# Gated cross-attention with a sparse FFN on one core: four engines in written order, and work placed between the seven products of each stage

## The chip, the core and the metric

The kernel runs on one core of a Trainium2 chip. A core has a matrix engine (TensorE, PE in the profile; its weight loads are listed as PEld), a vector engine (VectorE, DVE), a scalar engine (ScalarE, ACT), a general engine (GpSimd, POOL) and an engine that here issues nearly all data transfers (SyncE, SP). The metric is the device time of one execution in microseconds (us); several runs are given by their median.

## What is computed

The input x is 32 sequences of 64 tokens with 512 channels (2048 tokens). With `ctx` of the same shape, a bias and a mask per sequence:

```python
# cross-attention: 32 heads of 128
q = layernorm(x) @ Wq ; k = ctx @ Wk ; v = ctx @ Wv
score = where(mask, q k^T / sqrt(128) + bias, -inf)
x = x + tanh(g_xattn) * ((softmax(score) v) @ Wo)
# FFN on y = layernorm(x), 1792 hidden units in 56 blocks of 32
inter = y @ c1^T @ c2^T
idx = first argmax of each block of inter
x = x + tanh(g_ffn) * (relu(y . w1[idx]) @ w2t[idx])
```

The FFN is computed densely: all 1792 hidden values, each multiplied by 1 where it is the first maximum of its block and by 0 elsewhere.

## The kernel before

**Products by Strassen's scheme.** Each 512x512x512 product is done as seven products of half-size blocks instead of eight. The class `Seven` holds a matrix as four raw blocks and three sums of blocks: `sums_left` (L129) makes the sums of a weight on POOL, four operations that each read two SBUF operands; `sums_right` (L139) makes those of the other operand on DVE, also four. `product` (L156) writes one of the seven into a PSUM bank of the tag "mm" (four banks); it is eight matmul instructions in the trace, and a stage of seven is 56. `collect` (L172) adds a finished product to the result: the first is copied by ACT (L177), the others are added by DVE (L179 to L190), eight operations in a stage. The order is `ORDER = (0, 5, 1, 6, 4, 2, 3)`; `RAW_FIRST = (0, 1, 5, 6, 4, 2, 3)` begins with the two products that use raw blocks alone.

**Attention** runs over 4 blocks of 512 tokens and in each over 8 groups of 4 heads: 32 units, u = 0 to 31. A unit has the stages q and k (`project_q`, L284), `values` of the unit before (po, L378), `scores` (sc, L325), v, and `output_sums` of the unit before (pw, L400), whose seven products are summed over the groups of a block in `acc` (L401; for a block's first group ACT copies them, L399). Inside k, ahead of its fifth product, stands `transpose_probs` of the unit before (pt, L109; ACT copies the result, L365). `scores` adds the bias on DVE (L332), takes the maximum (L341), subtracts it (L342), has ACT take the exponential (L345), and DVE sums (L346), inverts (L347), masks (L349) and multiplies (L355). At a block's end POOL combines the seven sums (`finish_sums`, L407 to L413) and DVE adds the result to x (`finish_block`, L418). In a block's last unit the next block of x is normalised and transposed (`norm_block`, L277) and the next `ctx` is loaded.

**FFN**: for each of the 4 blocks of tokens, `ffn_rank` (pc, L458) and `ffn_eq` (pi, L485) compute `inter` in two small products, DVE takes each block's maximum (L498) and compares (L499), POOL multiplies by a rank (L500), DVE takes the maximum again (L503) and POOL subtracts (L504), so that the first maximum is left over. `ffn_hidden` (L511 to L567) computes the hidden units in four groups (512, 512, 512 and 256) as seven chains of matmuls each; `ffn_output` (fo, L582) multiplies by w2. pi uses the two PSUM banks of the tag "pv", from block 1 on also two of "mm".

**Order.** `manual_schedule` (L195) names PE and POOL: these two carry out their instructions in the order in which they are written. DVE, ACT and SP are ordered by the framework's scheduler, which may put an instruction ahead of one that is written earlier. Weights have one buffer each (tags wq, wk, wv, wo): the next unit's weight is issued on SP when the stage that used the buffer is over, and POOL makes its sums when it has landed. The bias tile has two buffers; POOL adds the mask to it (L303) in the unit that uses it. The first loads are issued on SP in the order ctx, wk, wv, x.

Of the kernel before, what the change touches and what calls it, by code (L numbers as in the profile page):

```python
# [23 lines left out]
P = 128  # L24
# [11 lines left out]
def kernel(  # L36
# [54 lines left out]

    def stats_of(pool, t0, n, name):
        st = pool.tile([P, n, 6], F32, tag=f"bnst{n}", name=f"st_{name}")
        mv = pool.tile([P, n, 2], F32, tag=f"bnmv{n}", name=f"mv_{name}")
        for i in range(n):
            nc.vector.bn_stats(st[:, i, :], xacc[:, t0 + i, :])
            nc.vector.bn_aggr(mv[:, i, :], st[:, i, :])
        return mv, rstd_of(pool, mv, n, f"rstd_{name}")
# [96 lines left out]
    with tc.manual_schedule(engines={mybir.EngineType.PE, mybir.EngineType.Pool}):  # L195

        def load_weight(tag, g):
            w = seven(wpool, tag, f"{tag}_{g}")
            src = {"wq": wq_d, "wk": wk_d, "wv": wv_d}.get(tag)
            if src is None:  # L200
                src = wo_d[ts(g % NHG, HG * DH), :]
            else:
                src = src[:, ts(g % NHG, HG * DH)]
            nc.sync.dma_start(w.raw, src.rearrange("(c p) n -> p c n", p=P))
            return w.sums_left(nc.gpsimd)

        def load_ctx(b):
            c = seven(att, "cT", f"cT_{b}")
            nc.sync.dma_start(
                c.raw, ctxT_d[:, ts(b, 512)].rearrange("(c p) t -> p c t", p=P)  # L210
            )
            return c

        make_identity(nc, ident)
        nc.vector.tensor_copy(identb, ident)
        nc.vector.memset(eps, EPS)
        nc.scalar.dma_start(gate[:, 0:1], gx_d.partition_broadcast(P))
        nc.scalar.dma_start(gate[:, 1:2], gf_d.partition_broadcast(P))
        nc.scalar.activation(tgx, gate[:, 0:1], AF.Tanh)
        nc.scalar.activation(tgf, gate[:, 1:2], AF.Tanh)  # L220

        cT = load_ctx(0)
        W = {"wk": load_weight("wk", 0), "wv": load_weight("wv", 0)}
        load_x(0, 2)
        load_x(2, 2)
        W |= {t: load_weight(t, 0) for t in ("wq", "wo")}
        for t in range(4, NTILE, 4):
            load_x(t, 4)
# [24 lines left out]
        class Norm:  # L253


            def __init__(self, b, name):
                self.b, self.name = b, name
                self.mv, self.rstd = stats_of(att, 4 * b, 4, f"{name}{b}")
                self.xn = {}

            def scale(self, *tiles):
                for i in tiles:
                    self.xn[i] = normalise(
                        att, 4 * self.b + i, self.mv, self.rstd, i, f"{self.name}{self.b}_{i}"
                    )

            def turn(self, *tiles):
                if 0 in tiles:
                    self.xT = seven(att, "xT", f"{self.name}xT_{self.b}")
                for i in tiles:  # L270
                    pt = ps_tr(f"{self.name}xt_{self.b}_{i}")
                    transpose4(pt, self.xn[i])
                    nc.scalar.copy(
                        self.xT.raw[:, :, ts(i, P)], pt.rearrange("p (k t) -> p k t", k=KC)
                    )

        def norm_block(b):  # L277
            n = Norm(b, "a")
            for i in range(4):
                n.scale(i)  # L280
                n.turn(i)
            return n.xT.sums_right(nc.vector)

        def project_q(u, w, src, name, mid=None, order=None):  # L284
            dst = att.tile([P, 2, 2, 512], F32, tag=name, name=f"{name}_{u}")
            pp = {}
            for n, i in enumerate(order or ORDER):
                if n == 4 and mid is not None:
                    mid()
                pp[i] = product(i, w, src, f"{name}_{u}_{i}", name != "v")  # L290
                if i == 1 and 5 not in pp:
                    continue
                collect(i, pp[i], dst)
                if i == 5 and 1 in pp:
                    collect(1, pp[1], dst)
# [17 lines left out]
        def scores(u, b, q, k, bt):  # L313
# [31 lines left out]
            nc.scalar.activation(pf, pf, AF.Exp)  # L345
            nc.vector.tensor_reduce(st[:, 1, :], pr, AX.X, ALU.add)  # L346
# [11 lines left out]
            return pf  # L358
# [34 lines left out]
        def output_sums(u, g, w, oT, acc, mid=None):  # L393
            for n, i in enumerate(ORDER):
                if n == 4 and mid is not None:
                    mid()
# [18 lines left out]
        def finish_block(b, acc):  # L415
            for i, r, half in ((1, 0, 0), (2, 0, 1), (3, 1, 0), (4, 1, 1)):
# [16 lines left out]
        def ffn_constants():  # L433
# [15 lines left out]
            nc.vector.tensor_copy(rank, rank_i)  # L449
            F.update(c2T=c2T, c1T=c1T, i1=i1, rank=rank)  # L450

        def ffn_rank(b):

            xT, i1 = F["norm"].xT, F["i1"]
            pc = ps_tr(f"pc_{b}")
# [15 lines left out]
        def ffn_eq(b, g, tiles, banks):  # L471
# [24 lines left out]
            for i, pi, ef in zip(tiles, pis, efs):  # L496
# [3 lines left out]
                nc.gpsimd.tensor_tensor(ef, ef, F["rank"][:, :n], ALU.mult)  # L500
            for i, ef in zip(tiles, efs):
# [18 lines left out]
        def ffn_hidden(b, g, mid1=None, mid2=None):  # L520
# [22 lines left out]
            nc.scalar.copy(h[0][1], view(X))  # L543

# [64 lines left out]

        cT.sums_right(nc.vector)  # L610
        k = project_q(0, W["wk"], cT, "k", order=RAW_FIRST)
        W["wk"] = load_weight("wk", 1)
        n = Norm(0, "a")
        n.scale(0, 1)

        def turn_first():
            n.turn(0, 1)
            n.scale(2, 3)
            n.turn(2, 3)

        v = project_q(0, W["wv"], cT, "v", turn_first, order=RAW_FIRST)
        xT = n.xT.sums_right(nc.vector)
        W["wv"] = load_weight("wv", 1)
        madd, seen = mask_block()
        prev = None
        acc = None
        U = NB * NHG
        done = None
        for u in range(U):
            b, g = divmod(u, NHG)  # L630
            mid = None
            if prev is not None:
                mid = lambda: transpose_probs(prev[0], prev[4])

            def queries(mid=None):
                q = project_q(u, W["wq"], xT, "q", mid)
# [6 lines left out]
            def keys(mid=None):  # L643
                k = project_q(u, W["wk"], cT, "k", mid)
# [6 lines left out]
            if u == 1:  # L651
                k = keys()
                q = queries(mid)
            else:
                q = queries()
                bt = load_bias(g, b)
                if g == NHG - 1 and b + 1 < NB:
                    xT = norm_block(b + 1)
                if u > 0:
                    k = keys(mid)  # L660
            if u == 1:
                bt = load_bias(g, b)
            if prev is not None:
                oT = values(prev[0], prev[3])
            if done is not None:
                finish_block(*done)
                done = None
            if u == U - 1:
                F["norm"] = Norm(0, "f")
                F["norm"].scale(0, 1)  # L670
            pf = scores(u, b, q, k, bt)
            if u > 0:
                v = project_q(u, W["wv"], cT, "v")
            if g == NHG - 1 and b + 1 < NB:
                cT = load_ctx(b + 1).sums_right(nc.vector)
            if u == U - 1:
                ffn_weight(2)
                ffn_constants()
                F["norm"].turn(0, 1)
                F["norm"].scale(2, 3)  # L680
            elif u > 0:
                W["wv"] = load_weight("wv", u + 1)
            if prev is not None:
                pu, pb, pg = prev[:3]
                if pg == 0:
                    acc = att.tile([P, 7, 512], F32, tag="acc", name=f"acc_{pb}")
                output_sums(
                    pu,
                    pg,
                    W["wo"],  # L690
                    oT,
                    acc,
                    (lambda: F["norm"].turn(2, 3)) if u == U - 1 else None,
                )
                if pg == NHG - 1:
                    finish_sums(acc)
                    done = pb, acc
                W["wo"] = load_weight("wo", u)
            prev = (u, b, g, v, pf)

        pv2 = (ps_pv, ps_pv)
        low, high = (0, 1), (2, 3)
        ffn_rank(0)
        transpose_probs(U - 1, pf)
        oT = values(U - 1, v)
        ffn_eq(0, 0, low, pv2)
        output_sums(U - 1, NHG - 1, W["wo"], oT, acc, lambda: ffn_eq(0, 0, high, pv2))
        ffn_weight(3)
        for b in range(NB):
            for g in range(4):  # L710
                m1 = m2 = None
                if b == 0 and g < 3:
                    m1 = lambda: ffn_eq(0, g + 1, low, pv2)
                    m2 = lambda: ffn_eq(0, g + 1, high, pv2)
                elif b > 0 and g < 2:
                    m1 = lambda: ffn_eq(b, 3, (low, high)[g], pv2)
                if g == 3 and b + 1 < NB:
                    F["norm"] = Norm(b + 1, "f")
                    F["norm"].scale(0, 1)
                ffn_hidden(b, g, m1, m2)  # L720
                if b == 0 and g == 0:
                    finish_sums(acc)
                    ffn_weights2(0)
                if b == 0 and g == 1:
                    finish_block(NB - 1, acc)
# [6 lines left out]
            more = b + 1 < NB  # L732
# [4 lines left out]
            for g in range(3):  # L737
                if more:
                    ffn_eq(b + 1, g, low + high, (ps_mm, ps_mm, ps_pv, ps_pv))
                if g < 2:  # L740
                    ffn_output(b, g + 2)
# [49 lines left out]
```

## Time and profile before

| | |
|---|---|
| median of 3 runs | 2267.83 us (2266.33 to 2271.6) |
| profiled execution, its own time | 2270.99 us |
| its span in the trace | 2269.2 us |
| mean granted TensorE clock | 0.989 |
| first matmul | 10.7 us into the span |
| PE busy | 2218.4 us, 98% |
| DVE, POOL, ACT busy | 53%, 41%, 15% |
| moved by DMA | 173.57 MB |

In the profile's lines a group of instructions is given as line, engine, operation, out<-in by the program's names, shapes and count; a timeline line begins with the start and the length in us, and ends, in brackets, with the engine's idle time before it and what ended it. A line of waits reads "engine line waited for: us in total, times, longest us". A line of the windows view gives a stretch, its length and the busy time and number of instructions of PE, PEld, DVE, ACT and POOL in it, then the granted TensorE clock (1 is full), the DMA engines' busy share and GB/s.

### The profile page before, as it was taken

What the parts mean: (1) busy time and instruction counts of PE and PEld (TensorE: products, weight loads), DVE (VectorE), ACT (ScalarE), POOL (GpSimd) and SP (SyncE); (2) the same over time, 40 slices, a digit from 0 to 9 for tenths busy, and PEclk for the clock granted to TensorE, in tenths of its full rate; (3) what the DMA queues carried; (4) which work ended last, traced back from release to release, by engine and by line L of the source; (5) the groups of instructions that cost most, each with busy time, mean ns of one, the idle gap of its engine ahead of it and who ended that gap; (6) DMA issues with size and microseconds to landing.
All of it is one profiled execution on the core that took longest, in us unless ns stands there. A gap on an engine that the chain in (4) does not pass through costs nothing.

```text
span 2269.2 us, 29536 instructions
## 1 busy us (share of the span) xinstructions
PE 2218.4 (98%) x12336; PEld 1857.3 (82%) x12336; DVE 1203.3 (53%) x1745; ACT 351.7 (15%) x572; POOL 931.8 (41%) x724
## 2 busy tenths in 40 slices
PE   7999999999999999999999999999999989999999
PEld 6788888888888888888888888888888865656574
DVE  6545555754555557545555565455555774545451
ACT  1211111211111112121111121211111211112020
POOL 5443344454344444544444445343334462313130
PEclk9999999999999999999999999999999999999999
DMA  6222222222222222222222232222222220000000
GB/s 246 75 84 84 88 95 87 102 84 66 89 95 87 84 84 103 84 82 86 84 84 84 84 103 84 84 84 84 87 94 80 65 75 10 10 13 7 15 5 19
DMA packets 88516, 173.57 MB, mean 76 GB/s; under 512 B 4480, under 2 KB 4992, under 8 KB 88384
## 3 DMA queue, kind: packets, MB, share of 16 engines
q1 hardware_dynamic: 87440, 171.19, 22.6%
q8 instruction: 98, 1.61, 0.3%
q10 hardware_dynamic: 944, 0.49, 0.1%
q14 instruction: 34, 0.28, 0.0%
HBM read 167.48 MB, written 4.19 MB: 76 GB/s over the span
## 4 chain that ended last, share of the span: by engine, by line
PE 92%; POOL 3%; DVE 2%; DMA 2%; issue 1%; ACT 0%; SPq 0%; POOLq 0%
PE v L163 17%; PE k L163 17%; PE q L163 16%; PE pw L163 15%; PE fo L582 9%; PE po L378 5%; PE hx L511 4%; PE sc L325 3%; PE hz L511 2%; PE pt L109 1%; PE hy L511 1%; PE pi L485 1%; DMA wv<-in_dram 1%; DVE xacc L418 1%; DMA wq<-in_dram 0%
## 5 line engine op out<-in xcount | busy, mean ns | idle before, releaser
L163 PE MATMUL q<-axT,wq 128*128 128x256 f32 x1792 | 400.9, 384 | 11.7 <-DVE q L179 9.6
L163 PE MATMUL k<-cT,wk 128*128 128x256 f32 x1792 | 399.1, 380 | 12.8 <-DMA wk<-in_dram 10.7
L163 PE MATMUL v<-wv,cT 128*128 128x256 f32 x1792 | 397.3, 382 | 1.9 <-DVE v L179 1.9
L163 PEld LDWEIGHTS q<-axT,wq 128*128 128x128 f32 x1792 | 344.8, 193 | 62.3 <-issue 14.3
L163 PE MATMUL pw<-wo,oT 128*128 128x256 f32 x1792 | 392.5, 379 | 0.0
L163 PEld LDWEIGHTS k<-cT,wk 128*128 128x128 f32 x1792 | 338.9, 191 | 58.1 <-issue 10.7
L163 PEld LDWEIGHTS v<-wv,cT 128*128 128x128 f32 x1792 | 338.9, 191 | 49.5 <-DVE v L179 2.3
L163 PEld LDWEIGHTS pw<-wo,oT 128*128 128x128 f32 x1792 | 340.2, 190 | 47.6 <-issue 0.8
L401 DVE TENSOR_TENSOR acc<-pw,acc 128x512 f32<-128x512 f32 x196 | 134.2, 690 | 156.6 <-PE pw L163 156.4
L132 POOL TENSOR_TENSOR wv<-wv 128x512 f32<-128x512 f32 x32 | 41.4, 1295 | 378.0 <-DMA wv<-in_dram 365.7
L582 PE MATMUL fo<-w,hT 128*128 128x512 f32 x448 | 195.8, 594 | 0.0
L582 PEld LDWEIGHTS fo<-w,hT 128*128 128x128 f32 x448 | 83.9, 190 | 104.7 <-issue 102.2
L132 POOL TENSOR_TENSOR wq<-wq 128x512 f32<-128x512 f32 x32 | 42.6, 1332 | 225.2 <-DMA wq<-in_dram 192.0
L132 POOL TENSOR_TENSOR wk<-wk 128x512 f32<-128x512 f32 x32 | 48.0, 1499 | 188.1 <-DMA wk<-in_dram 157.5
L378 PEld LDWEIGHTS po<-pbd,v 128*128 128x128 f32 x1024 | 121.7, 192 | 3.4 <-ACT pbd L365 1.0
L378 PE MATMUL po<-pbd,v 128*128 128x128 f32 x1024 | 123.0, 278 | 0.6 <-ACT pbd L365 0.6
L132 POOL TENSOR_TENSOR wo<-wo 128x512 f32<-128x512 f32 x32 | 40.5, 1266 | 186.3 <-DMA wo<-in_dram 133.1
L500 POOL TENSOR_TENSOR eqa<-eqa,ffn_const 128x512 bf16<-128x512 bf16 x32 | 37.0, 1165 | 181.6 <-DVE eqa L499 180.9
L511 PE MATMUL hx<-fxT,w 128*128 128x256 f32 x448 | 109.2, 389 | 0.0
L511 PEld LDWEIGHTS hx<-fxT,w 128*128 128x128 f32 x448 | 87.3, 196 | 17.4 <-issue 4.9
L387 ACT COPY oT<-po 128x512 f32<-128x512 f32 x128 | 74.9, 585 | 159.0 <-PE po L378 158.9
L365 ACT COPY pbd<-pt 64x512 f32<-64x512 f32 x128 | 74.2, 579 | 159.5 <-PE pt L109 151.4
(144 smaller groups left out, 2528.4 us busy)
## 6 DMA issues: line engine op xcount, KB each, us to landing
wk<-in_dram SPq DMA_DIRECT2D x32, 1024.0 KB, 5.3
wv<-in_dram SPq DMA_DIRECT2D x32, 1024.0 KB, 5.5
wq<-in_dram SPq DMA_DIRECT2D x32, 1024.0 KB, 5.3
wo<-in_dram SPq DMA_DIRECT2D x32, 1024.0 KB, 5.4
bias<-in_dram SPq DMA_DIRECT2D x64, 256.0 KB, 2.8
cT<-in_dram SPq DMA_DIRECT2D x4, 1024.0 KB, 5.3
out_dram<-xacc SPq DMA_DIRECT2D x16, 256.0 KB, 2.0
w<-in_dram SPq DMA_DIRECT2D x2, 1792.0 KB, 8.4
```

Source lines behind the costliest of these rows:

```text
L109: nc.tensor.transpose(pt[:, ts(k, P)], src[:, ts(k, P)], ident)
L132: eng.tensor_tensor(s1, a21, a22, ALU.add)
L163: nc.tensor.matmul(pp[:, ts(j, HALF)], a[:, kc, ts(j, P)], b[:, kc, :], start=(kc == 0), stop=(kc == 1),)
L325: nc.tensor.matmul(sc[ts(r, S), ts(col, S)], q[:, hp, half, tok : tok + S], k[:, hp, half, tok : tok + S], start=True, stop=True,)
L365: nc.scalar.copy(pbd[ts(c, S), ts(half, 8), c, :], pt[ts(c, S), :].rearrange("p (a q) -> p a q", q=S),)
L378: nc.tensor.matmul(po[:, ts(2 * j + i, P)], v[:, r, half, i * HALF + j * P : i * HALF + (j + 1) * P], pbd[:, ((2 * half + i) * 2 + r) * 2 ...
L387: nc.scalar.copy(oT.raw[:, 2 * r : 2 * r + 2, ts(half, HALF)], po.rearrange("p (j t) -> p j t", j=2),)
L401: nc.vector.tensor_tensor(acc[:, i], pw, acc[:, i], ALU.add)
L418: nc.vector.scalar_tensor_tensor(a, acc[:, i].rearrange("p (i n) -> p i n", i=2), tgx, a, ALU.mult, ALU.add,)
L500: nc.gpsimd.tensor_tensor(ef, ef, F["rank"][:, :n], ALU.mult)
L511: nc.tensor.matmul(pp[:, ts(j, HALF)], s[:, kc, ts(j, P)], t[:, kc, :], start=(first and j == 0 and kc == 0), stop=(j == nj - 1 and kc == ...
L582: nc.tensor.matmul(po, F["hT", c // 4][:, c % 4, ts(i, P)], F["w2"][c // 7][:, c % 7, :], start=(c == 0), stop=(c == NIC - 1),)
```

## The change

All four compute engines follow the written order, and each stage takes a dictionary of hooks: work that is written ahead of its n-th product. `norm_block` and `stats_of` become the methods `stats`, `scale` and `turn` of `Norm`, spread over q and k of a block's last unit; `scores` ends with the exponential, and the rest, `divide`, stands ahead of v's third product; `finish_block` is cut into four parts in k and v; `ctx`'s sums move into q of the next block's first unit; the bias is loaded and masked one unit ahead; the last steps of `ffn_eq` (`ffn_first`) are put off until the next call or `ffn_ties`; the FFN's first `ffn_rank` and `ffn_eq` move into pw of unit 30; from block 1 on group 3's `ffn_eq` moves to later places; and the first ctx and wk are loaded in halves of their columns, wk from ACT's queue. The tanhs of the gates and the bf16 identity move behind unit 0's scores.

```diff
-    with tc.manual_schedule(engines={mybir.EngineType.PE, mybir.EngineType.Pool}):
+    with tc.manual_schedule(
+        engines={
+            mybir.EngineType.PE,
+            mybir.EngineType.Pool,
+            mybir.EngineType.DVE,
+            mybir.EngineType.Activation,
+        }
+    ):
...
+            if parts is None:
+                nc.sync.dma_start(w.raw, src)
+                return w.sums_left(nc.gpsimd)
+            for cols in parts:
+                nc.scalar.dma_start(w.raw[:, :, cols], src[:, :, cols])
+            return w
...
+        halves = (slice(0, HALF), slice(HALF, 512))
+        cT = load_ctx(0, halves)
+        W = {"wk": load_weight("wk", 0, halves)}
+        load_x(0, 4)
         make_identity(nc, ident)
         nc.vector.memset(eps, EPS)
+        W["wk"].sums_left(nc.gpsimd)
+        W |= {t: load_weight(t, 0) for t in ("wv", "wq", "wo")}
...
-        def project_q(u, w, src, name, mid=None, order=None):
...
+        def project(u, w, src, name, hooks=None, order=None):
+
             dst = att.tile([P, 2, 2, 512], F32, tag=name, name=f"{name}_{u}")
             pp = {}
             for n, i in enumerate(order or ORDER):
-                if n == 4 and mid is not None:
-                    mid()
+                call(hooks, n)
                 pp[i] = product(i, w, src, f"{name}_{u}_{i}", name != "v")
...
             nc.scalar.activation(pf, pf, AF.Exp)
+            return pf, pr, st
+
+        def divide(b, pr, st):
             nc.vector.tensor_reduce(st[:, 1, :], pr, AX.X, ALU.add)
...
+            ffn_ties()
+            F["ties"] = lambda: ffn_first(b, g, tiles, efs, nb, blocks, over)
...
+            hq, hk, hv, hp = {}, {}, {}, {}
             if prev is not None:
-                mid = lambda: transpose_probs(prev[0], prev[4])
+                turn_probs = lambda: transpose_probs(prev[0], prev[4])
+                (hq if u == 1 else hk)[4] = turn_probs
+            if last:
+                F["norm"] = norm = Norm(b + 1, "a") if more else Norm(0, "f")
+                for i in range(4):
+                    hq[i + 2] = lambda i=i: norm.stats(i)
+                hk[0] = lambda: norm.scale(0, 1)
+                hk[1] = lambda: norm.turn(0)
+                hk[2] = lambda: (norm.turn(1), norm.scale(2, 3))
+                hk[3] = lambda: norm.turn(2)
+                hk[5] = lambda: norm.turn(3)
+                if more:
+                    hp[1] = lambda: norm.xT.sums_right(nc.vector)
+                else:
+                    hp[4] = lambda: ffn_rank(0)
+                    hp[6] = lambda: ffn_eq(0, 0, low, pv2)
+            if g == 0 and u > 0:
+                hq[3] = lambda: cT.sums_right(nc.vector)
+            if done is not None:
+                hk[5] = lambda: finish_block(*ended, (0,))
+                hk[6] = lambda: finish_block(*ended, (1,))
+                hv[5] = lambda: finish_block(*ended, (2,))
+                hv[6] = lambda: finish_block(*ended, (3,))
...
+            pf, pr, st = scores(u, b, q, k, B_.pop(u))
+            bias(u + 1)
+            hv[2] = lambda: divide(b, pr, st)
             if u > 0:
-                v = project_q(u, W["wv"], cT, "v")
+                v = project(u, W["wv"], cT, "v", hv)
...
-        ffn_eq(0, 0, low, pv2)
-        output_sums(U - 1, NHG - 1, W["wo"], oT, acc, lambda: ffn_eq(0, 0, high, pv2))
-        ffn_weight(3)
+        ffn_eq(0, 0, high, pv2)
+        output_sums(
+            U - 1,
+            NHG - 1,
+            W["wo"],
+            oT,
+            acc,
+            {
+                2: lambda: ffn_eq(0, 1, low, pv2),
+                5: lambda: ffn_eq(0, 1, high, pv2),
+            },
+            RAW_FIRST,
+        )
...
+                    if g == 0:
+                        m1 = lambda: (ffn_eq(0, 2, low, pv2), ffn_weight(3))
+                        m2 = lambda: (
+                            ffn_eq(0, 2, high, pv2),
+                            finish_sums(acc),
+                            ffn_weights2(0),
+                        )
+                    if g == 2:
+                        m1 = lambda: finish_block(NB - 1, acc, (0, 1))
+                        m2 = lambda: finish_block(NB - 1, acc, (2, 3))
+                    ties = (0, 0, 2, 3)[g]
+                else:
+                    if g == 0:
+                        m2 = lambda: ffn_eq(b, 3, low, pv2)
+                    if g == 1:
+                        m1 = lambda: ffn_eq(b, 3, high, pv2)
+                        m2 = ffn_ties
+                if more and g == 3:
                     F["norm"] = Norm(b + 1, "f")
-                    F["norm"].scale(0, 1)
-                ffn_hidden(b, g, m1, m2)
+                    m1 = lambda: F["norm"].stats(0, 1, 2, 3)
+                    m2 = lambda: F["norm"].scale(0, 1)
+                ffn_hidden(b, g, m1, m2, ties)
```

## The prediction

> **What bounds the kernel now.** I read the page first, then what TensorE (PE) waits for, its clock over stretches, and the timeline of one unit. Section 1 of the page:
>
> ```profile
> PE 2218.4 (98%) x12336; PEld 1857.3 (82%) x12336; DVE 1203.3 (53%) x1745; ACT 351.7 (15%) x572; POOL 931.8 (41%) x724
> ```
>
> PE is the bound, and no matmul is removed. In a steady unit it has no gap: in the chain, v of units 5 and 6 starts at 312.13 and 367.24, 55.11 us apart, each 56-matmul stage 12.1 us, each of its seven products 1.73. Only PE's waits can be won. The longest, with us in total, times, longest:
>
> ```profile
> PE pi L485 <- DVE eqb L499: 16.8, 7, 7.6
> PE k L163 <- DMA wk<-in_dram: 10.7, 1, 10.7
> PE q L163 <- DVE q L179: 9.6, 3, 3.2
> ```
>
> A wait can cost more than its length. Two neighbouring stretches of unit 1 (PE busy, then PEclk, third from the right):
>
> ```profile
> 96.60:99.40 2.80, 0.90 (x5) 0.74 (x5) 2.77 (x4) 0.00 (x0) 0.00 (x0) 1.00 0.49 181
> 99.50:102.80 3.30, 3.30 (x9) 2.59 (x9) 3.30 (x7) 1.06 (x1) 0.00 (x0) 0.50 0.00 1
> ```
>
> After a wait of 1.90 us the clock is half for 3.4 us. The same view of the FFN: from the last attention sums to group 2; group 0 of block 1; its group 1:
>
> ```profile
> 1784.97:1866.70 81.73, 72.39 (x362) 56.11 (x361) 58.68 (x87) 17.78 (x30) 49.76 (x42) 0.94 0.26 83
> 1943.99:1964.99 21.00, 17.83 (x80) 14.17 (x77) 13.55 (x24) 4.20 (x6) 10.95 (x12) 0.84 0.04 13
> 1964.99:1978.86 13.87, 13.87 (x78) 11.72 (x77) 6.92 (x14) 4.20 (x6) 2.44 (x4) 1.00 0.00 0
> ```
>
> The stage on which I think the change turns is v. Unit 5, then unit 9, in the timeline:
>
> ```profile
> 311.75 1.44 POOL L132 TENSOR_TENSOR wk<-wk 128x512 f32<-128x512 f32 x1 [5.28 <-DMA wk<-in_dram]
> 311.99 1.76 DVE L145 TENSOR_TENSOR oT<-oT 128x512 f32<-128x512 f32 x1
> ...
> 312.06 12.35 PE L163 MATMUL v<-wv,cT 128*128 128x256 f32 x56
> ...
> 314.10 0.58 ACT L177 COPY v<-v 128x512 f32<-128x512 f32 x1 [3.35 <-PE v L163]
> ...
> 316.07 1.27 POOL L135 TENSOR_TENSOR wk<-wk 128x512 f32<-128x512 f32 x1
> 316.23 2.19 DVE L342 TENSOR_TENSOR prob<-prob,sst 128x1024 f32<-128x1024 f32 x1
> 318.35 0.68 DVE L179 TENSOR_TENSOR v<-v,v 128x512 f32<-128x512 f32 x1
> 318.52 1.06 ACT L345 ACTIVATE prob<-prob 128x1024 f32<-128x1024 f32 x1 [3.84 <-DVE prob L342]
> ```
>
> ```profile
> 541.97 0.68 DVE L145 TENSOR_TENSOR oT<-oT 128x512 f32<-128x512 f32 x1
> 542.18 1.60 POOL L132 TENSOR_TENSOR wk<-wk 128x512 f32<-128x512 f32 x1 [5.67 <-PE sc L325]
> ...
> 547.54 1.06 ACT L345 ACTIVATE prob<-prob 128x1024 f32<-128x1024 f32 x1 [2.88 <-DVE prob L342]
> ```
>
> See the copy of v's first product (L177) standing well ahead of the exponential, and a DVE operation with two SBUF inputs (L145, L342) waiting out the POOL operation in flight (2.19 us, where L355 of the same shape, free of POOL, takes 1.22). If POOL starts wk's sums before L145 (18 of units 1 to 31), the exponential comes 6.45 us after v's start; if after (13), 5.5.
>
> **The change part by part.**
>
> *v stage.* `scores` writes the exponential ahead of v, so ACT in written order can't copy v's first product until it is done; and DVE does the whole of `divide` before it collects the third. Four banks hold the products: the fifth needs the first's bank, the seventh the third's. Before, the fifth starts at 7.01 and the seventh at 10.46 us after v's start, unhindered. Late form: exponential at 6.45, copy behind it from 7.41 to 7.99, fifth product at 8.03: 1.02 lost. DVE then: collect (L179) at 8.02, sum (L346) at 8.62, reciprocal 1.25 later, then 0.28, 0.21 and 1.14 (spacings of unit 1's rows) to the collect at 11.50, done 12.18; seventh product at 12.22, not 11.48: 0.74. Sum 1.76. Early form: copy done at 7.03, so 0.06, then 0.74: 0.80. In all 18 x 1.76 + 13 x 0.80 = **+42.1**. Behind the waiting copy on ACT stands nothing else; DVE's collects wait for it. Units 7, 15 and 23 show a table load (1.28) between subtraction and exponential, and unit 31 now gets one, its square root having moved ahead: 4 x 1.28 = **+5.1**.
>
> Do these waits cool the clock? The Trainium skill ("TensorE: Matmul & The Clock Gate", Part 1: The HAM clock gate) has the clock fall only after an idle window of about 3.4 us: then no. The row above contradicts it, 1.90 us sufficed; yet a wait of 2.10 at 64.5 did not cool. Waits of 1.02 and 0.74 lie far under both: nothing. Units 7 and 31 wait about 2.3: half of 2 x 1.7 (3.4 us at half clock): **+1.7**; by the page 0.
>
> *Block ends.* v to v across units 8-9, 16-17, 24-25 takes 62.25, 62.39, 60.50 in the chain against 55.11: 19.8 too much, because DVE sits in `finish_block` (L418) for POOL's sums while q's products wait. Now its four parts stand in k and v of that unit, some 10 us after POOL's seven sums, one behind each product. The transposes' waits go too (3 x 0.46). **-21.2**. New is `cT.sums_right` in q of the next block's first unit: four two-input operations meet wo's four POOL sums (454.74 to 459.81 in unit 8) and alternate with them, about 1.25 + 0.6 each, so that q's fourth product is collected 1.7 us after k's first needs its bank: 3 x 1.7 = **+5.0**. The hooks in unit 7's q and k (statistics, scaling, transposes) leave DVE 1.6 us of work per 1.73 us product and stay inside the four-bank slack; xn may be 0.1 late: **+0.3**.
>
> *FFN.* Group 0 of blocks 1 to 3 takes 21.0, 20.4 and 19.5 us, an undisturbed group with one pair of pi 13.9: 19.3 lost to pi waiting for DVE's comparison and to the half clock after it. The pair moves some 8 us later, when DVE's four comparisons (5.6 us) are over: **-19.3**. Against it, group 3 of blocks 0 to 2 now holds the next block's statistics: DVE 4 x 0.92 from 0.85 us into the group, the square root on ACT to 4.9, and behind it on ACT the copy L543 that the sixth chain waits for: that at 5.25 instead of 3.96, and 0.43 more behind the Relu: 3 x 1.73 = **+5.2**.
>
> Transition: pw of unit 31 starts 23.8 us after pw of unit 30, as now (23.7). From there 12.1 for pw, 2.1 for two pi pairs and 1.4 for the first of them (its banks are still being compared), 15.3 for group 0, 14.3 for group 1: 45.2. DVE lags, but `finish_block` no longer stands before a pi. 23.8 + 45.2 = 69.0 against 81.7, less 0.9 of transposes moved into k: **-11.8**.
>
> *Start.* The first two products need only first halves. On one queue 1.02 MB had landed at 7.0 us and 2.07 MB at 10.0. A second queue (ACT) carries wk. The skill ("Trainium Kernel Development and Optimization", Key Constraints) says that queues share the same 16 engines and only issue time is saved: then PE starts at about 7.3, but the third product needs two POOL sums (1.3 each) of the whole wk, at 13.0 instead of 15.93: **-2.9**. If queues added up, about -5. A 512 KB load in 1 KB packets took 5.0 us beside another: then 0. Bias one unit ahead takes away POOL's late addition in units 0 and 1 (losses of 2.4 + 0.7 + 0.2 and 3.85); 1.1 comes back, since k of unit 1 waits behind unit 0's exponential and tanhs: **-6.0**.
>
> *At nothing.* Ties (`ffn_first`) deferred: POOL and DVE work behind chains that need it a group later; uncovered, one call's four reductions cost 2.8. `ffn_rank` comes 6.9 us into pw of unit 30, and its constants landed 6.9 us after issue on ACT's queue, behind which no product waits: 0.2 at most. w1's last group is loaded two pi later, needed three groups on. The second half of w2 is issued after `finish_block`'s last part: 8.4 us to land against about 12 of PE work; uncovered, 1 to 4. Bias on POOL after wk's sums: it ends 8.9 us into v, DVE's next two-input operation comes at 9.2. SP's order stays the scheduler's; the mask load could come late at 3 us. The moved pi, transposes and copies are the same instructions.
>
> Sum: 42.1 + 5.1 + 1.7 - 21.2 + 5.0 + 0.3 - 19.3 + 5.2 - 11.8 - 2.9 - 6.0 = **-1.8 us**. Span 2269.2 becomes 2267.4. The profiled execution took 2270.99, 1.8 outside the span, 3.2 above the median 2267.83. So the median becomes 2266.0.
>
> **Rivals.**
> 1. *Faster: the exponential in its early form everywhere.* wk's landing and L145 are 0.3 us apart; if wk lands a little later, all 31 units lose 0.80: 17 us less, 2249. Should wk's sums miss the softmax altogether, v's waits vanish and it is 2224. Against: SP issues wk at the same point of k.
> 2. *Slower: the late form everywhere.* The other side of the same 0.3 us: 13 x 0.96 = 12.5 more, 2278. It counts as slower from 25 late units of 31 on (7 more than 18: -1.8 + 6.7 = +4.9).
> 3. *Gains not had*: the hooks put as much DVE work before other banks. With half of the FFN's and blocks' 42 us (net) lost, 2287; with a quarter, 2276. For it: DVE is busy 58.7 of the transition's 81.7 us.
> 4. *It does nothing*: written order equals the scheduler's in q, k, pw. Against: L177 and L345 do change places.
>
> **How the numbers follow.** My forecast (-12 to +6 about -1.8) 0.45; rival 1 0.20; rival 2 0.12; rival 3 0.20; rival 4 0.03. Within 0.2% (4.5 us, about what a measurement tells from no change): 0.18 of the forecast, rival 4, a little of the rest: 0.22. Faster: 0.21 of the forecast, rival 1: 0.41. Slower: 0.06 of the forecast, rivals 2 and 3 nearly whole: 0.37. The range takes in rival 1's first case and most of rivals 2 and 3: 2246 to 2284; the forecast's own is 2256 to 2274.
>
> **What would show it.** In v: L177 directly after L345 on ACT, L181 after L355 on DVE, and waits of v on ACT v L177 (about 24 us in total) and on DVE v L181 (about 23). v to v across block ends near 57, steady units 55.9 or 56.9. `pi` waits gone from block 1 on; a wait of hx on ACT hT in groups 3. First matmul near 7.3 us. Steady units still 55.1 apart would prove the v step wrong, and the time would be near 2224.

## The result, and the profile after

The changed kernel takes 2285.99 us (median of 6 runs, 2280.97 to 2288.08), the kernel before beside it 2268.66 (6 runs): ratio 1.0067, 95% interval 1.005 to 1.0084. It is slower, clear of the scatter, and 2 us above the range. The profiled execution took 2288.08 us with a span of 2286.3; the prediction's sum stood at a span of 2267.4, so 18.9 us are to be explained. No work was added: PE is busy 2222.8 us (2218.4 before).

What PE waits for after the change (engine, line, releaser: us in total, times, longest); the lines of v are new, and `pi` has shrunk from 16.8 to 1.2:

```profile
PE v L155 <- ACT v L169: 20.4, 19, 2.1
PE v L155 <- DVE v L173: 14.1, 29, 0.5
...
PE hx L528 <- ACT hT L560: 5.9, 3, 2.0
PE k L155 <- DVE k L171: 4.6, 1, 4.6
PE k L155 <- DVE q L175: 3.1, 3, 1.1
...
PE pi L495 <- DVE eqa L509: 1.2, 2, 0.9
```

The timeline of a late unit, 6, whose v starts at 372.19 (line numbers are those of the changed kernel: L137 is L145 of before, L349 was L342, L352 was L345, L169 was L177):

```profile
372.06 1.27 POOL L124 TENSOR_TENSOR wk<-wk 128x512 f32<-128x512 f32 x1 [7.80 <-DMA wk<-in_dram]
372.11 1.76 DVE L137 TENSOR_TENSOR oT<-oT 128x512 f32<-128x512 f32 x1
...
376.36 2.19 DVE L349 TENSOR_TENSOR prob<-prob,sst 128x1024 f32<-128x1024 f32 x1
...
378.64 1.06 ACT L352 ACTIVATE prob<-prob 128x1024 f32<-128x1024 f32 x1 [7.77 <-DVE prob L349]
379.60 0.57 ACT L169 COPY v<-v 128x512 f32<-128x512 f32 x1
...
380.22 3.72 PE L155 MATMUL v<-wv,cT 128*128 128x256 f32 x16 [0.85 <-ACT v L169]
...
383.69 0.68 DVE L173 TENSOR_TENSOR v<-v,v 128x512 f32<-128x512 f32 x1
...
384.43 0.92 PE L155 MATMUL v<-wv,cT 128*128 128x256 f32 x3 [0.49 <-DVE v L173]
```

The copy of the first product now follows the exponential, and 0.05 us after it the fifth product starts (8.03 us into v); the seventh starts when L173, DVE's collect of the third, has given its bank back (12.24). The prediction had 8.03 and 12.22.

Unit 1's key stage, where the prediction had a gain. First the windows view of the stretch after its long wait (the granted clock is the third number from the right), then the timeline between 57 and 66 us:

```profile
65.80:72.00 6.20, 6.17 (x15) 4.88 (x16) 3.25 (x5) 0.00 (x0) 0.00 (x0) 0.50 0.00 0
```

```profile
57.96 0.56 ACT L169 COPY k<-k 128x512 f32<-128x512 f32 x1
...
59.44 1.08 DVE L359 TENSOR_TENSOR sst<-sst,seen 128x16 f32<-128x16 f32 x1
...
60.55 2.24 DVE L365 TENSOR_TENSOR prob<-prob,sst 128x1024 f32<-128x1024 f32 x1
61.67 3.32 POOL L310 TENSOR_TENSOR bias<-bias,madd 128x1024 f32<-128x1024 f32 x1
62.72 2.36 DVE L743 CAST identb<-ident 128x128 bf16<-128x128 f32 x1
65.00 0.68 DVE L171 TENSOR_TENSOR k<-k,k 128x512 f32<-128x512 f32 x1
...
65.83 1.62 PE L155 MATMUL k<-cT,wk 128*128 128x256 f32 x3 [4.64 <-DVE k L171]
```

The copy from ACT is there at 58.52, but the collect L171 comes at 65.00. Ahead of it on DVE stand unit 0's divide and the copy of the identity, both written at the end of unit 0, and both stretched by POOL's operations beside them: the cast of 128x128 elements takes 2.36 us (0.22 before). PE waits 4.64 us and then runs 6.2 us at half clock.

Where the span went, by the start of each stage's first matmul. The prediction's column comes from its terms: 82.7 = 87.8 - 2.9 - 3.3 + 1.1; 1710.3 = 1684.1 - 3.85 + 40.3 + 3.8 + 0.9 - 21.2 + 5.0 + 0.3 + 0.9; 109.8 = 116.9 + 1.8 + 1.3 + 0.8 - 12.7 + 1.7; 312.7 = 328.5 - 19.3 + 3.5.

| stretch | before | predicted | after | missed by |
|---|---|---|---|---|
| start to v of unit 1 | 87.8 | 82.7 | 91.1 | 8.4 |
| v of unit 1 to v of unit 31 | 1684.1 | 1710.3 | 1713.8 | 3.5 |
| v of unit 31 to the first fo | 116.9 | 109.8 | 114.3 | 4.5 |
| first fo to that of block 3 | 328.5 | 312.7 | 314.6 | 1.9 |
| from there to the span's end | 51.9 | 51.9 | 52.5 | 0.6 |

### The profile page after: what moved, and what is told of

Its sections match the earlier page's. It is cut to its first block, busy times and chain, and to the rows that moved or that the text cites. A ratio compares the mean times of both kernels' runs of the same rounds, so it can differ in the third digit from the quotient of the medians.

```text
span 2286.3 us, 29580 instructions
## 1 busy us (share of the span) xinstructions
PE 2222.8 (97%) x12336; PEld 1845.0 (81%) x12336; DVE 1222.6 (53%) x1745; ACT 351.2 (15%) x574; POOL 950.8 (42%) x724
## 4 chain that ended last, share of the span: by engine, by line
PE 77%; DVE 17%; ACT 3%; issue 2%; POOL 1%; DMA 0%; DVEq 0%; ACTq 0%; POOLq 0%; SPq 0%
PE pw L155 17%; PE k L155 17%; PE q L155 15%; PE fo L601 8%; PE po L387 5%; PE hx L528 4%; PE v L155 4%; DVE prob L349 3%; PE hz L528 2%; DVE oT L137 2%; DVE sst L348 2%; DVE prob L339 2%; DVE prob L365 2%; DVE sst L356 1%; ACT prob L352 1%
## 5 line engine op out<-in xcount | busy, mean ns | idle before, releaser
L155 PE MATMUL v<-wv,cT 128*128 128x256 f32 x1792 | 413.8, 387 | 34.5 <-ACT v L169 20.4
L155 PE MATMUL k<-cT,wk 128*128 128x256 f32 x1792 | 405.8, 383 | 14.9 <-DMA wk<-in_dram 6.2
L155 PE MATMUL q<-xT_a,wq 128*128 128x256 f32 x1792 | 392.4, 379 | 0.0
L155 PEld LDWEIGHTS pw<-wo,oT 128*128 128x128 f32 x1792 | 342.1, 191 | 50.6 <-issue 1.7
L155 PEld LDWEIGHTS q<-xT_a,wq 128*128 128x128 f32 x1792 | 340.3, 190 | 46.5 <-issue 0.3
L124 POOL TENSOR_TENSOR wv<-wv 128x512 f32<-128x512 f32 x32 | 40.6, 1268 | 332.0 <-DMA wv<-in_dram 270.1
L124 POOL TENSOR_TENSOR wk<-wk 128x512 f32<-128x512 f32 x32 | 47.4, 1482 | 255.6 <-DMA wk<-in_dram 186.6
L124 POOL TENSOR_TENSOR wq<-wq 128x512 f32<-128x512 f32 x32 | 41.9, 1309 | 208.8 <-DMA wq<-in_dram 208.8
L124 POOL TENSOR_TENSOR wo<-wo 128x512 f32<-128x512 f32 x32 | 40.8, 1274 | 190.4 <-DMA wo<-in_dram 130.3
L528 PE MATMUL hx<-xT_f,w 128*128 128x256 f32 x448 | 107.2, 384 | 5.9 <-ACT hT L560 5.9
L169 ACT COPY q<-q 128x512 f32<-128x512 f32 x32 | 18.8, 586 | 551.2 <-PE q L155 551.2
L528 PEld LDWEIGHTS hx<-xT_f,w 128*128 128x128 f32 x448 | 84.8, 191 | 22.7 <-ACT hT L560 7.1
```

What stands on the lines that cost most here:

```text
L124: eng.tensor_tensor(s1, a21, a22, ALU.add)
L155: nc.tensor.matmul(pp[:, ts(j, HALF)], a[:, kc, ts(j, P)], b[:, kc, :], start=(kc == 0), stop=(kc == 1),)
L528: nc.tensor.matmul(pp[:, ts(j, HALF)], s[:, kc, ts(j, P)], t[:, kc, :], start=(first and j == 0 and kc == 0), stop=(j == nj - 1 and kc == ...
```

## The experiments

My theory: the written order costs about 50 us in the v stages (exponential ahead of the first copy, divide ahead of the third collect), the gains elsewhere are real, and the rest of the miss lies in unit 1 and in the FFN's group 3. Rivals: POOL's sums of wk alone make the loss; the placement is the loss; the loss lies outside the v stages. Unless said otherwise each kernel is the changed one with one edit; times are medians, beside 2267.7 to 2270.3 for the kernel before. A step is the time from one unit's v to the next unit's.

**1. The exponential behind the first copy.**

```diff
-            nc.scalar.activation(pf, pf, AF.Exp)
             return pf, pr, st
...
+            exponent = lambda: nc.scalar.activation(pf, pf, AF.Exp)
+            hv[1] = exponent
             hv[2] = lambda: divide(b, pr, st)
...
+                hv[1]()
                 hv[2]()
```

> Edit: in each v stage the exponential is written behind the ScalarE copy of the first product (hook 1) instead of ahead of it; the divide stays at hook 2. My theory (the exponential ahead of the copy, and the divide ahead of the third collect, are what the written order costs): the 19 waits of v's fifth product for the copy at L169 (20.4 us in all) go; VectorE's first collect no longer waits for that copy, so the sum over the exponentials starts at 6.5 us after v's start in the early units (7.66 now) and 7.5 in the late ones (8.6): the seventh product's wait goes in the early units and about 0.7 us of it stays in the late ones. Time about 2286 - 35 = 2251 us. Rival A (the late or early case is set by POOL's sums of wk beside VectorE, the order does not matter): the waits move to the divide, seventh product still near 12.2 us in late units, time above 2275. Rival B (the loss lies at the start, the transition and the FFN, not in the v stages): above 2280.

Measured: 2258.89 us (ratio to before 0.996, 0.9951 to 0.9968). The waits for the copy are gone, but the seventh product still waits, 31 times (19.1 us): it starts at about 10.8 us into v in 9 early units, 11.17 in 18 late ones and 12.44 in the 4 late ones with a table load, 10.46 being unhindered. Right in kind; 27 us less instead of 35: the early units keep 0.33 us, 22 units were late in this execution, not 18, and the table loads still cost.

**2. The divide later.**

```diff
-            hv[2] = lambda: divide(b, pr, st)
+            hv[4] = lambda: divide(b, pr, st)
...
-                hv[2]()
+                hv[4]()
```

> Edit: the divide is written ahead of v's fifth product (hook 4) instead of the third (hook 2); the exponential stays ahead of the copy. My theory: the waits of the seventh product for L173 (29 times, 14.1 us) go, the waits of the fifth for L169 stay (about 1.0 us in the 18 late units). A unit's step falls from 56.03 to about 55.2 us in early units and from 56.98 to about 56.2 in late ones: about 24 us less, 2262 us. Rival A (a divide of 3 us of VectorE work is in the way wherever it is put, its wait only moves to the first products of the output stage): 2280 or more, with waits of pw for L175 or L178 of about the same sum. Rival B (loss is elsewhere): above 2280.

Measured: 2258.88 us (0.9974, 0.9955 to 0.9993). The waits for L173 are gone, those for the copy stay (18.6 us), early steps take 55.3 and late ones 56.2. The 3 us of divide are in nobody's way at hook 4, so rival A falls.

**3. Both edits.**

> Edit: both, the exponential behind the first copy (hook 1) and the divide at hook 4. My theory: v's products run without a wait, steps from v to v near 55.1 us as before the change, and what the change gains at the block ends, in the FFN and at the transition stays: 2286 less about 46 for the v stages less 4 for half clock and table loads behind the waits, so 2234 to 2240 us, faster than the kernel before (2269). Rival A (other work of the written order then becomes the next wait, in the query, key or output stages): 2255 to 2275. Rival B (loss elsewhere): above 2280.

Measured: 2232.46 us (0.986, 0.9845 to 0.9875), span 2229.8. The longest waits of PE in it, but for the first load's:

```profile
PE hx L527 <- ACT hT L559: 5.9, 3, 2.0
PE k L155 <- DVE k L171: 4.1, 1, 4.1
PE k L155 <- DVE q L175: 2.9, 3, 1.0
```

No v is left in the list, and steady steps are 55.11 again. From v of unit 1 to v of unit 31 it takes 1663.9 us: 49.8 less than the changed kernel, and 20.2 less than the kernel before, which is what the other terms of the prediction (block ends, ctx's sums, unit 1's second part) give for this stretch (18.9). The loss is the order in v, and the gains are real.

**4. POOL's sums of wk written behind v.**

```diff
-                return w.sums_left(nc.gpsimd)
+                return w.sums_left(nc.gpsimd) if sums else w
...
-                    W["wk"] = load_weight("wk", u + 1)
+                    W["wk"] = load_weight("wk", u + 1, sums=False)
...
+                    W["wk"].sums_left(nc.gpsimd)
                     W["wv"] = load_weight("wv", u + 1)
```

> Edit: only POOL's four sums of the next wk are moved, from behind the key stage to behind the v stage (their load stays); the exponential and the divide stay as in the changed kernel. My theory: those sums beside VectorE's sums of oT and its subtraction are what makes a unit late (L137 ends at 1.68 instead of 0.6 us after v's start), so all 31 units become early: step 56.03, about 18 x 0.95 = 17 us less, 2269 us, with the half clock of units 7 and 23 gone 2266; the early units' loss of 0.9 us stays. Rival A (late or early has another cause): no change, 2286. Rival B (POOL's sums are as much in the way of VectorE's additions in the output stage): 2290 or more.

Measured: 2285.93 us (1.0088, 1.0067 to 1.0109): nothing. It didn't test what it was meant to: POOL had nothing else queued, so the sums began when wk had landed, 0.14 us before v's start in unit 2 and 0.02 before it in unit 4, as always. Unit 2 was late, unit 4 early, and 16 of the 31 were late. A place in the order is no time; what had to be moved was the load (experiment 9).

**5. Unit 0's divide and identity copy behind unit 1's key collects.**

```diff
+                hk[6] = lambda: (
+                    divide(b, pr, st),
+                    nc.vector.tensor_copy(identb, ident),
+                )
                 k = keys()
...
-                hv[2]()
                 nc.scalar.activation(tgx, gate[:, 0:1], AF.Tanh)
                 nc.scalar.activation(tgf, gate[:, 1:2], AF.Tanh)
-                nc.vector.tensor_copy(identb, ident)
```

> Edit: unit 0's divide and the bf16 copy of the identity are taken from the end of unit 0 and written at hook 6 of unit 1's key stage; all else as in the changed kernel. Theory (unit 1's key products wait because VectorE's collects stand behind unit 0's divide, which runs beside POOL's sums of wq and its addition of the bias): the wait of 4.64 us and the half clock after it (3.1 us) go; unit 1's v starts near 83.5 us instead of 91.1, time about 2286 - 7.5 = 2278.5 us. Rival A (the bias, one unit ahead, is what holds the key stage: POOL's addition is late whatever VectorE does): v of unit 1 still after 89 us, 2284 to 2286. Rival B (the wait moves to the key stage's last products or to the query stage): v of unit 1 at 86 to 89 us.

Measured: 2278.01 us (1.0027, 1.0018 to 1.0036), 8 us less. The timeline:

```profile
60.32 0.56 ACT L169 COPY k<-k 128x512 f32<-128x512 f32 x1
...
60.91 0.69 DVE L171 TENSOR_TENSOR k<-k,k 128x512 f32<-128x512 f32 x1 [1.78 <-ACT k L169]
```

The collect follows the copy at once, the divide ends only at 69.2, and PE has no wait and no half clock between unit 0's scores and unit 1's. v of unit 1 starts at 85.86, and not at 83.5, because this execution lost 2.6 us more than the changed kernel's between 25 and 32 us; in experiment 11, with the same edit, it starts at 83.42.

**6. The FFN's statistics in group 2.** `stats` for the next block goes from group 3's first middle to group 2's two middles; the square root stays in group 3.

> Edit: in the FFN the next block's statistics (VectorE) are written in the middles of group 2 instead of group 3; the square root stays at group 3's first middle. Theory (statistics and square root ahead of group 3's collects cost 1.97 us of wait in each of blocks 0 to 2 and some clock after it): the three waits of hx for L560 (5.9 us) go, about 3 us more of clock with them, time 2286 - 7 to 9 = 2277 to 2279 us. Rival A (group 2 of block 0 holds the last block end as well, so the wait moves there): 2282. Rival B (the same VectorE work is in the way in any group): 2286.

Measured: 2274.11 us (1.0021, 1.0012 to 1.003). The three waits of hx are gone; from v of unit 31 to the first fo it takes 110.2 us instead of 114.3, from there to block 3's 309.5 instead of 314.6. So 9.2 us in place; the 12 of the medians contain scatter (2269 to 2282).

**7. DVE and ACT left to the scheduler, all placement kept.**

```diff
-    with tc.manual_schedule(
-        engines={
...
-            mybir.EngineType.DVE,
-            mybir.EngineType.Activation,
-        }
-    ):
+    with tc.manual_schedule(engines={mybir.EngineType.PE, mybir.EngineType.Pool}):
```

> Edit: one line: the changed kernel with only TensorE and POOL in written order; VectorE and ScalarE take the scheduler's order again, placement and loads stay as changed. Theory (the written order of ScalarE and VectorE in the v stage is the loss, and the placement, the bias and the loads are the gain): v runs without waits as in the kernel before, steps near 55.1, time 2235 to 2250 us. Rival A (the placement is the loss, the order does nothing): 2280 or more. Rival B (the scheduler cannot use the placement, its block ends wait as before): about 2265.

Measured: 2245.51 us (0.9887, 0.9872 to 0.9901). v has no wait and steady steps take 55.11; but the block ends take 61.15, 60.49 and 62.23 as before, with a wait that the changed kernel does not have:

```profile
PE q L155 <- DVE q L171: 12.7, 4, 3.2
```

So the placement is not the loss, and the two halves of the change pull in opposite directions: written order is what takes away the 18.5 us above 55.11 at the block ends, and what loses 50 in v.

**8. The order alone**: the kernel before, with the same four engines named, nothing moved.

> Edit: one line: the kernel before with all four compute engines in written order; nothing is moved. Theory (the written order costs where the text puts work ahead of a collect): in the kernel before the exponential and the whole divide stand in the text ahead of all of v's collects, so v's fifth product waits several us in each of 31 units, and the norms at the block ends are written in one piece: 60 to 200 us more, 2330 to 2470 us. Rival (the order as such does little, since the scheduler's was nearly the same): within 20 us of 2269.

Measured: 2411.87 us (1.0615, 1.0599 to 1.063).

```profile
PE v L163 <- ACT v L177: 44.6, 20, 6.2
PE v L163 <- DVE v L179: 29.7, 24, 1.2
```

The same two lines of v lead. The change's hooks had taken away most of what the order costs, and not all.

**9. wk's load, and so POOL's sums of it, behind v.**

```diff
-                if u + 1 < U:
-                    W["wk"] = load_weight("wk", u + 1)
-                else:
+                if u + 1 == U:
                     ffn_weight(1)
...
                     W["wv"] = load_weight("wv", u + 1)
+                    W["wk"] = load_weight("wk", u + 1)
```

> Edit: in units 1 to 30 the load of the next wk, and with it POOL's sums of it, is issued behind the v stage instead of behind the key stage; exponential and divide stay where the changed kernel has them. The run before it that moved only the sums moved nothing on the chip: POOL had nothing else to do, so they began when the load landed, 0.1 us from v's start as before. With the load moved, no POOL work lies beside VectorE's fourth sum of oT, its reduction and its subtraction. Theory (POOL's sums beside VectorE's two-input operations make a unit late and slow the subtraction from 1.22 to 2.2 us): L137 ends at 0.6 us after v's start in every unit, the subtraction takes 1.22 us, the exponential ends near 5.5 us; the copy at L169 waits no one, and the seventh product's wait falls below 0.3 us: 30 to 40 us less, 2245 to 2256 us. Rival A (late and early have another cause): both kinds of unit stay, 2280 or more. Rival B (the sums now lie beside the output stage's additions, and the next key stage waits for wk): v stages as the theory says but 2265 or more, with waits of k for POOL.

Measured: 2240.71 us (0.9876, 0.9857 to 0.9895). Unit 9, whose v starts at 538.11:

```profile
538.03 0.68 DVE L137 TENSOR_TENSOR oT<-oT 128x512 f32<-128x512 f32 x1
...
541.20 1.22 DVE L349 TENSOR_TENSOR prob<-prob,sst 128x1024 f32<-128x1024 f32 x1
542.52 1.06 ACT L352 ACTIVATE prob<-prob 128x1024 f32<-128x1024 f32 x1 [5.74 <-DVE prob L349]
543.48 0.57 ACT L169 COPY v<-v 128x512 f32<-128x512 f32 x1
```

With no POOL work beside it the subtraction takes 1.22 us instead of 2.19 or 2.3, in all of units 2 to 30, and the copy, still behind the exponential, is done 5.9 us into v, before anyone needs it. That is 45 us less, against 53 in experiment 3, from the other end: the loss in v needs both, the order and POOL's sums. (Units 1 and 31 still meet POOL's sums, and the table loads of units 7, 15 and 23 still cost.) This is the 2224 us that the prediction's first rival named ("wk's sums miss the softmax altogether"), plus the misses outside the v stages (8.4 + 4.5 + 1.9 + 0.6 = 15.4 in the table).

**10. The first loads whole again**, on the same two queues.

> Edit: the first context tile and the first wk are loaded whole again, one transfer each, on the two queues that the changed kernel uses; all else as changed. Theory (the halves let the first product start when half of the columns are there, but the third product waits for the second halves, so the halves alone are worth little): the first product starts 2 to 4 us later than 6.2 us, v of unit 0 at 22 to 23 us instead of 21.7, total within 2 us of 2286. Rival (the halves are what brings the start forward): v of unit 0 at 24 us or later, 2288 or more.

Measured: 2281.91 us (1.0053, 1.0034 to 1.0071). The first product starts at 9.12 instead of 6.23 us and v of unit 0 at 23.83 instead of 21.72 (24.56 before): the halves are worth 2.1 us there, what else changed at the start 0.7. In this execution the wait of unit 1 (3.8 us) was followed by no half clock, so v of unit 1 came at 89.56, earlier than with halves. So the halves do more than I expected, nearly what the rival said (24). The total lies under both forecasts and doesn't tell the two apart: this execution is also without the half clock that the changed kernel's had in unit 1 and in the transition.

**11. Experiments 3, 5 and 6 together.**

> Edit: three of the former edits together: exponential behind the first copy and divide at hook 4 in the v stages (alone: 2232.5), unit 0's divide and identity copy in unit 1's key stage (alone: 7.9 less), the FFN's statistics in group 2 (alone: 11.9 less, in a median of scattered runs; 5.9 us of waits). Theory (the three losses are independent): 2232.5 - 7 - 8 = about 2217 us, 2213 to 2221. Rival (one of them was hidden behind another): 2222 to 2232.

Measured: 2216.24 us (0.9766, 0.9747 to 0.9785). The three losses add up.

**12. And the last two waits**: ctx's sums one by one at hooks 2 to 5, the transition's `ffn_eq` at hooks 3 and 6.

> Edit: as the one with three edits, and the four sums of a new context tile are written one by one at hooks 2 to 5 of the query stage instead of together at hook 3, and the transition's rank work at hooks 3 and 6 instead of 2 and 5. Theory (four sums together ahead of a collect hold it up by 1.0 us at each of three block starts; the transition's 0.9 us wait and the half clock of about 5 us after it come from rank work written too close together): 3 us less for the first, 0 to 5 for the second, about 2211 us. Rival (the wait only moves to the FFN's first middle): as with three edits, or 2 us more.

Measured: 2209.76 us (0.9736, 0.9716 to 0.9757): 2.6% faster than the kernel before. The longest waits left:

```profile
PE k L159 <- DMA wk<-in_dram: 6.3, 1, 6.3
PE xt_a L101 <- DVE xn_a L94: 1.3, 2, 0.8
```

From v of unit 1 to v of unit 31 it takes 3.3 us less than in experiment 11 (three block starts), from there to the first fo 1.6 less.

## Why the prediction was wrong, step by step

*Unit 1, the step that failed most.* "1.1 comes back, since k of unit 1 waits behind unit 0's exponential and tanhs." What came back was 7.9 (k of unit 1 takes 20.1 us, and 12.2 in experiment 11): 4.6 of wait, 3.1 of half clock and 0.2 not placed. I had followed ACT's order there and not DVE's: of the divide that moved with the exponential, only v's places were costed, and in unit 0 there is no v behind which it could stand. On top, the bias "one unit ahead" puts POOL's addition of 3.32 us just beside that divide. About 1.1 us more of the 8.4 went at the first transposes, which wait for DVE's normalisation. Experiment 5 gave 8 us back.

*v stage: right in mechanism, 5 us short in size.* Between v of unit 1 and v of unit 31, the terms of the sum (waits, table loads, clock) made 45.0 us; undoing the order gave 49.8. The count of late and early units (18 and 13) and the starts of the fifth and seventh products held. Short were the price of a step, 0.92 early and 1.87 late instead of 0.80 and 1.76 (from the seventh product to the stage's end PE took 1.99 us instead of 1.89), and the clock: units 7 and 23 each lost about 1.0 us to half clock after a wait of 2.1, where the sum had 0.85, for unit 7. (The half clock itself takes 1.8 us, but 0.8 of it is the seventh product's wait, which then falls away.) That POOL's sums make a unit late was an inference from two rows; experiment 9 showed it.

*Clock after waits.* The prediction weighed the Trainium skill's idle window of about 3.4 us ("TensorE: Matmul & The Clock Gate", The HAM clock gate) against a row of 1.90, and gave units 7 and 31 half of the cost each. What came was the full cost in units 7 and 23 and none in unit 31: a sum about right by luck. In all 14 traces a half clock inside the span lasts 3.41 us, or two or three times that, and within a trace the half clocks begin whole multiples of 3.41 us apart, so stretches of that length can be laid on this grid. Here are two for unit 7 and three for unit 31 of the changed kernel, then three for unit 1 of experiment 10 (length, PE busy first; the clock third from the right):

```profile
437.22:440.63 3.41, 1.28 (x7) 0.80 (x6) 0.47 (x2) 2.81 (x3) 2.27 (x1) 1.00 0.00 0
440.63:444.04 3.41, 3.41 (x10) 2.70 (x9) 3.31 (x6) 0.00 (x0) 0.00 (x0) 0.50 0.00 0
1809.38:1812.79 3.41, 2.63 (x13) 1.97 (x11) 1.81 (x1) 1.51 (x2) 0.73 (x1) 1.00 0.01 2
1812.79:1816.20 3.41, 2.05 (x10) 1.82 (x11) 2.04 (x3) 1.30 (x2) 0.00 (x0) 1.00 0.00 0
1816.20:1819.61 3.41, 2.92 (x14) 2.26 (x13) 3.24 (x7) 0.00 (x0) 0.00 (x0) 1.00 0.00 0
```

```profile
62.03:65.45 3.42, 1.50 (x7) 0.97 (x6) 3.39 (x3) 0.00 (x0) 3.42 (x2) 1.00 0.00 0
65.45:68.86 3.41, 1.52 (x7) 1.40 (x8) 3.20 (x5) 0.00 (x0) 1.06 (x1) 1.00 0.00 0
68.86:72.27 3.41, 3.41 (x18) 3.00 (x17) 2.41 (x4) 0.00 (x0) 0.00 (x0) 1.00 0.05 6
```

Unit 7's wait of 2.13 us lies in one stretch and leaves PE 1.28 us of work in it; unit 31's of 2.14 is shared by two, with 2.63 and 2.05. The wait of 3.8 in experiment 10 is cut in two by a border, and the clock stays; the 4.64 of the changed kernel emptied a whole stretch. In the transition two waits of 0.94 and 0.23 us, with the small pi products between them, were followed by half clock too:

```profile
1847.30:1856.70 9.40, 8.23 (x18) 4.79 (x17) 9.12 (x15) 0.00 (x0) 8.22 (x8) 0.66 0.00 0
```

By the page this costs nothing. The stretch ahead of it (from 1846.93) has PE busy for 2.24 us, but only 0.71 without the pi products, which use 16 of 128 rows (the lines have "16*128"). Counting a pi product as an eighth, over all 14 traces from 15 us on: half clock followed every one of the 70 stretches at full clock that were busy for less than 0.43 of their length, 3 of 9 between 0.43 and 0.46, and none of some 9040 above. A stretch need not be idle, then, as the page has it, and a wait's length alone doesn't decide: where it falls on the grid does as well. This is a count, not an experiment; the weight of pi is an assumption that fits.

From pw of unit 31 to group 2 the chip took 50.6 us, the sum 45.2, which held 1.4 of wait and no clock: 5.4 short, of which 6.8 us at half clock make 3.4. In experiment 12, without these waits, the stretch took 45.4 at a clock of 1.00.

*Group 3 of the FFN.* 3 x 1.73 was forecast; measured were waits of 1.97, 1.96 and 1.97, and experiment 6 gave back 4.1 in the first case (some half clock among it) and 2.6 in each of the others. The mechanism was right (square root ahead of the copy on ACT), the size 4 short.

*What held.* Block ends: 56.02, 56.99 and 56.03, of which the v step is 0.9 or 1.9, so the whole excess over 55.11 is gone (-19.8). FFN groups 0 of blocks 1 to 3: 13.97. v of unit 0 earlier by 2.84, for 2.9: its k stage's third product starts at 12.98, 13.0 being forecast for POOL's sums, so the first product, at 6.23 instead of 7.3, gained nothing more. ctx's sums were dear at 3 x 1.7: 3 x 1.0. The rivals: neither "early everywhere" nor "late everywhere" came, and rival 3, gains not had, was wrong too, though its time (2287) was close: the gains were had, and new losses stood beside them.

## What to carry to other kernels

When an engine goes into written order, list for every bank or buffer the one instruction that frees it, and read what is written ahead of that instruction on its engine, in the first and the last unit as well as in the steady one. Only work that is ready by then may stand ahead of it; here two lines moved, or one load, turned 0.7% slower into 1.2 to 1.4% faster. What begins when a transfer lands is moved by moving the transfer, not its line.

## What the runs showed of the hardware

- A CAST of one SBUF operand (L743) took 2.36 us beside POOL's bias addition (3.32 us) and 0.22 without it (experiment 5); I had expected that only of DVE operations with two SBUF inputs. Of these, even one of 128x16 elements (L359) took 1.08 instead of 0.17, beside one of POOL's sums.
- Whether a unit was late turned on which came first, L124 on POOL or L137 on DVE, within some 0.1 us: 18, 22 and 16 late units in three executions of near kernels.
- By 5.0 us of the span 0.36 MB had landed before the change, 0.98 MB after it and 0.94 MB with whole loads: with the first loads on two queues and ahead of everything else they come about 2 us earlier, and the first product started at 6.23 where 7.3 was forecast. Whether the second queue or the order does it was not tried.
- Half clock came in units of 3.41 us on a fixed grid, and after stretches of that grid in which PE was busy for less than about 0.45 of the time, the small products counted by their rows: so after a wait of 2.13 us and not after one of 3.8 in another execution.
